# A selective scan with its partitions ordered state by state instead of channel by channel

## The chip, the cores and the metric

The kernel runs on one core of a Trainium2 chip, in float32 throughout. The metric is the device time of one execution in microseconds; less is better. A core has five engines with instruction streams of their own: PE multiplies matrices, ACT applies functions and copies, DVE and POOL work elementwise, SP issues DMAs here. They wait for each other through semaphores. Sixteen DMA engines move data between the on-chip memory (128 partitions) and DRAM.

## What is computed

Two layers on an input of [2, 256, 256, 128]: an attention over the first image axis, then a state space layer, each on a group-normalised input and added to its input. The change touches the second one alone. Cut to what matters (C = 128 channels, DI = 256 inner channels, 16 states, L = 65,536 positions per image):

```python
xi, z = split(gn(x) @ in_proj_w.T)                  # 256 channels each
xi = silu(depthwise_conv3x3(xi) + conv_b)           # xs, [B, 256, L]
dts, Bs, Cs = split(x_proj_w @ xs)                  # 8, 16 and 16 rows
delta = softplus(dt_w @ dts + dt_b)                 # [B, 256, L]
A = -exp(A_logs)                                    # [256, 16]
for t in range(L):                                  # per channel d and state n
    h[d, n] = exp(delta[d, t] * A[d, n]) * h[d, n] + delta[d, t] * xs[d, t] * Bs[n, t]
    y[d, t] = sum over n of h[d, n] * Cs[n, t]
y = y + Ds * xs
out = x + (layernorm(y) * ln_g + ln_b) * silu(z) @ out_proj_w.T
```

## The kernel before

**Stages.** After set-up and statistics comes attention; its result `x1` goes to DRAM. The scan stage then works through 128 steps (`steps`), 64 for each of two images; a step is R = 4 image rows, T = 1,024 positions.

**The partitions of a scan.** A step has 256 channels x 16 states = 4,096 recurrences of T positions, and one scan instruction runs 128 of them, one per partition. So a step has NU = 32 units: a unit takes CQ = 32 channels (one of four quarters `q` of one of two halves `h`) and SR = 4 states (one of four groups `m`). In the kernel before partition p holds channel p // 4 and state p % 4. Two units with neighbouring quarters form a pair (`PAIRS`, line 655). A pair's place in that tuple gives its time: unit t begins at slot t, and a step has 32 slots.

**Spreading the operands.** What the scan needs per partition is fetched from DRAM copies with repetition. `spread` (line 1154) fetches 32 channel rows of `delta_d` or `du_d` and repeats each for 4 states; `repeat` (line 1149) fetches 4 state rows of `bc_d` (B or C) and repeats them for 32 channels. Each such fetch fills a [128, 1024] tile. Per step there are 8 fetches of delta (`fetch_delta`, five buffers), 8 of du (`fetch_du`, two per tile, two buffers), 5 of B, 5 of C (`fetch_b`, `fetch_c`, two buffers each) and one of the fourth group of C (`fetch_cx`). All DMAs are issued by SP.

**The work of a unit.** `decay` (1229): ACT forms exp(delta x A), with A as a per-partition scale `a_neg`, in a PSUM tile `da`. `drive` (1241): POOL multiplies du and B for a pair at once. `scan` (1269): DVE runs the recurrence, with the end of the last step as its start. `remember` (1277): ACT keeps the last column. The product with C is made by DVE for single units (`product`, 1286) or by POOL for the eight pairs in `POOLED` (`products`, 1294). `add_up` (1316): PE sums over the 4 states with a 128 x 32 selection matrix `sel`, into 32 rows of `y`.

**The turned state group.** For the fourth group (`TURNED`) the drive is made another way, to spare POOL. `turn_du` (960) transposes du so that positions lie on partitions; `turn_du_out` (969) copies it into `zt`; `drives` (974) writes three copies of it scaled with B of one state each, the fourth being scaled through C. `turn_in` (1257) transposes 128 columns of `zt` back into `da`. `zt` is laid out as

```python
v["zt"] = s6.tile([P, T // P, DI, SR], F32, name="zt")
nc.scalar.copy(v["zt"][:, 2 * i : 2 * i + 2, :, SR - 1], o["ut", i])
```

so a copy of one state (256 elements, lines 976 to 981) reads and writes every fourth element, 16 bytes apart.

**Projecting ahead and finishing.** `project` (769) prepares a step up to 52 slots early: load four rows, `turn` and `normalise` them to channels on partitions (`xn`), `inner` and `conv`, `gate`, `silu`, `states`, `size`, `softplus`, `times`; it stores sz, xs, delta, du and B/C rows to DRAM. `begin` (793) keeps two rows of the step before or, on an image's first step, clears the row above the image, loads its first row into a tile `ob` and turns it; after the image's last row it clears a row. `finish_row` (1024) takes one of four rows of the step before through layer norm, gating, output projection and the store.

**The order.** Nothing is reordered by a scheduler in this stage: every piece has times in the table `TIMES` (line 661), in slots relative to the step's first unit, `at` (747) adds 32 slots per step, and all pieces are issued in the order of these times (lines 1385 to 1387). So each engine's stream, SP's too, is the order of the table.

**Set-up that depends on the partition order.** `sel` (152) sums the identity's columns in groups of 4. `same` (172), which has 1 where p % 32 = c, serves the convolution's weights. `A_logs` goes through a DRAM tile `alog_d` (190) in 32 small DMAs, to be read back with (channel, state) as partition.

Of the kernel before, what the change touches and what calls it, by code (L numbers as in the profile page):

```python
# [9 lines left out]
F32 = mybir.dt.float32  # L10
AF = mybir.ActivationFunctionType
ALU = mybir.AluOpType
AX = mybir.AxisListType
# [3 lines left out]
P = 128  # L17
# [5 lines left out]
def attn_then_ssm_kernel(  # L23
# [26 lines left out]
    nc = tc.nc  # L50
    B, H, W, C = x.shape
# [54 lines left out]
    first = ExitStack()  # L106
# [3 lines left out]
    for k in range(2):  # L110
# [40 lines left out]
    a_neg = const.tile([P, NCG, NSG], F32, name="a_neg")  # L151
    sel = const.tile([P, CQ], F32, name="sel")
    nc.vector.tensor_reduce(
        sel, ident.rearrange("p (c r) -> p c r", r=SR), AX.X, ALU.add
    )

    RB = TB // W
# [1 line left out]
    with tc.tile_pool(name="prep", bufs=1) as prep, tc.tile_pool(  # L159
# [7 lines left out]
        for r in range(RB):  # L167
            for dy in range(3):
                nc.sync.dma_start(
                    out=cw[(r + dy) * CQ : (r + dy + 1) * CQ, :, r, :], in_=taps[:, :, dy, :]  # L170
                )
        same = prep.tile([P, CQ], F32, name="same")
        nc.vector.tensor_reduce(
            same, ident.rearrange("p (r c) -> p c r", c=CQ), AX.X, ALU.add
        )
        nc.vector.tensor_tensor(
            w_cv.rearrange("p g r d c -> p (g r d) c"),
            same.unsqueeze(1).to_broadcast([P, NCG * RB * 3, CQ]),
            cw.rearrange("p g r d -> p (g r d)").unsqueeze(2).to_broadcast([P, NCG * RB * 3, CQ]),
            ALU.mult,  # L180
        )
# [5 lines left out]
        nc.sync.dma_start(out=xpw[32:64, :], in_=x_proj_w[0, DR : DR + 2 * NS, :])  # L187
        dtw = prep.tile([P, NH, DR], F32, name="dtw")
        nc.sync.dma_start(out=dtw, in_=dt_w[0].rearrange("(h p) r -> p h r", p=P))
        alog_d = dram.tile([CQ, SR, NCG, NSG], F32, name="alog_d")  # L190
        for g in range(NCG):
            for m in range(NSG):
                nc.sync.dma_start(
                    out=alog_d[:, :, g, m],
                    in_=A_logs[g * CQ : (g + 1) * CQ, m * SR : (m + 1) * SR],
                )
        alog = prep.tile([P, NCG, NSG], F32, name="alog")
        nc.sync.dma_start(out=alog, in_=alog_d.rearrange("c r g m -> (c r) g m"))
        a_pos = prep.tile([P, NCG, NSG], F32, name="a_pos")
        nc.scalar.activation(a_pos, alog, AF.Exp)  # L200
        nc.vector.tensor_scalar(a_neg, a_pos, -1.0, None, ALU.mult)
# [116 lines left out]
    with ExitStack() as actx:  # L318
# [268 lines left out]
        with tc.manual_schedule(engines=engines):  # L587
# [71 lines left out]
    POOLED = (2, 4, 10, 12, 18, 20, 26, 30)  # L659
    SUMS = ((0, 2), (4, 6), (8, 10), (12, 14), (16, 18), (20, 22), (24, 26), (28, 30))  # L660
    TIMES = {
        "add_up": (6.724, 10.523, 15.234, 17.357, 23.577, 27.066, 31.528, 34.187,),
        "begin": (-46.647,),
        "conv": (-37.319, -33.26, -30.256, -23.187,),
        "conv_out": (-37.203, -32.298, -29.079, -22.531,),
        "decay": (
            -0.457, -0.009, 1.46, 2.524, 2.97, 3.951, 4.748, 6.603, 7.256, 7.99, 7.7, 8.96, 9.084,
            7.786, 12.346, 13.841, 15.488, 16.811, 17.403, 14.296, 19.264, 20.338, 21.36, 21.952,
            23.923, 24.277, 25.955, 26.637, 26.688, 28.054, 29.215, 30.729,
        ),  # L670
        "drive": (
            -2.478, -0.654, 1.762, 3.81, 6.989, 11.716, 14.121, 17.755, 19.949, 23.283, 25.806,
            26.998,
        ),
        "drives": (
            -8.898, -8.755, 2.16, 8.854, -5.671, -4.828, -5.842, -1.931, -5.258, 3.165, -5.885,
            6.474, 2.13, 5.925, -3.57, 1.156,
        ),
        "fetch_b": (-4.274, -3.132, 4.233, 5.726, 22.495,),
        "fetch_c": (-2.23, 2.972, 5.721, 10.592, 28.034,),  # L680
        "fetch_cx": (-6.513,),
        "fetch_delta": (-9.068, -2.243, 0.347, -2.618, 11.064, 13.651, 5.759, 10.856,),
        "fetch_du": (-5.916, -3.021, 10.561, 13.429,),
        "gate": (-33.667, -30.07, -30.491, -26.072,),
        "gate_out": (-33.279, -28.439, -30.401, -25.691,),
        "inner": (-40.499, -39.775, -36.487, -34.84, -31.681, -31.179, -27.674, -24.89,),
        "inner_out": (-39.934, -39.214, -35.665, -34.411, -31.186, -30.784, -27.39, -23.412,),
        "load": (-52.341,),
        "normalise": (-43.293, -42.071,),
        "product": (  # L690
            0.814, 1.744, 6.726, 7.428, 8.79, 9.803, 15.226, 15.302, 17.41, 17.593, 23.225,
            23.505, 24.863, 25.246, 28.32, 29.93,
        ),
        "products": (5.397, 7.89, 14.546, 17.263, 21.546, 22.117, 27.902, 34.092,),
        "remember": (
            1.264, 2.345, 3.214, 6.053, 6.484, 7.988, 9.009, 9.1, 11.486, 14.169, 14.492, 15.761,
            17.254, 17.474, 20.057, 21.886, 23.549, 23.215, 25.088, 26.351, 27.149, 29.047,
            30.658, 32.752,
        ),
        "row_back": (41.992, 49.875, 57.857, 65.191,),  # L700
        "row_fetch": (43.062, 45.977, 52.544, 63.797,),
        "row_gated": (44.51, 49.95, 58.115, 65.232,),
        "row_leave": (45.329, 51.392, 61.182, 70.675,),
        "row_mix": (44.946, 51.011, 60.158, 69.774,),
        "row_norm": (41.251, 49.16, 55.004, 63.737,),
        "row_scales": (41.007, 47.422, 54.441, 63.428,),
        "row_stats": (39.857, 46.949, 53.374, 62.217,),
        "row_turn": (39.103, 45.623, 53.215, 61.229,),
        "silu": (-20.93,),
        "size": (-17.158, -16.246, -14.523, -14.865,),  # L710
        "size_out": (-16.533, -15.379, -13.973, -14.754,),
        "softplus": (-12.917,),
        "start_up": (-5.227, 19.105,),
        "start_up_y": (6.598, 23.449,),
        "states": (-20.725, -18.696,),
        "states_out": (-19.252, -17.616,),
        "times": (-11.031,),
        "turn": (-44.119, -42.473,),
        "turn_b": (-13.925,),
        "turn_b_out": (-12.571,),  # L720
        "turn_du": (-9.691, -6.021, -7.213, -4.676,),
        "turn_du_out": (-9.002, -5.843, -7.087, -4.562,),
        "turn_in": (9.374, 10.415, 10.881, 11.321, 17.974, 18.627, 19.701, 20.235,),
        "y_out": (20.647, 36.827,),
    }
    IN_F = {"gate": (0, 1, 0, 0), "turn_du": (2, 2, 2, 3)}
    s1 = ctx.enter_context(tc.tile_pool(name="s1", bufs=1))
# [41 lines left out]
    def project(k):  # L769
# [23 lines left out]
        def begin():  # L793
            if s == 0:
                if k > 0:
                    nc.gpsimd.memset(xn[:, 0, :], 0.0)
                first = s1.tile([P, WT, C], F32, name="ob")
                nc.sync.dma_start(
                    out=first, in_=x1[b][0].rearrange("(t p) c -> p t c", p=P)
                )  # L800
                o["first"] = first.unsqueeze(1)
                turn("first", 0, 1)
                normalise(1, 1)
            else:
                nc.scalar.copy(xn[:, 0:2, :], xn[:, R : R + 2, :])
            if n < R:
                nc.gpsimd.memset(xn[:, 2 + n, :], 0.0)

        def turn(src, r, m):
            t_ps = o["t"] = bank([P, RB, W], "t_ps")  # L810
            for i in range(m):
                for t in range(WT):
                    nc.tensor.transpose(
                        t_ps[:, i, t * P : (t + 1) * P], o[src][:, r + i, t, :], ident
                    )

        def normalise(to, m):
            nc.scalar.activation(
                xn[:, to : to + m, :],
                o["t"][:, 0:m, :],  # L820
                AF.Identity,
                bias=sh,
                scale=rs,
            )

        def inner(h, i, j, f=0):

# [140 lines left out]

        def turn_du_out(i):
            if i == 0:  # L970
                v["zt"] = s6.tile([P, T // P, DI, SR], F32, name="zt")
            nc.scalar.copy(v["zt"][:, 2 * i : 2 * i + 2, :, SR - 1], o["ut", i])  # L972

        def drives(j, n, m):
            for r in range(n, m):
                nc.scalar.activation(  # L976
                    v["zt"][:, j, :, r],
                    v["zt"][:, j, :, SR - 1],
                    AF.Copy,
                    scale=v["bt"][:, j, r : r + 1],  # L980
                )
# [167 lines left out]
    def repeat(k, name, row, m, pool):  # L1149
        tl = repeats[name, k, m] = pool.tile([P, T], F32, name=name[:3].rstrip("'"))  # L1150
        a = row + m * SR
        nc.sync.dma_start(out=tl, in_=given[k]["bc"][a : a + SR, :].partition_broadcast(CQ))

    def spread(k, name, tl, h, q):
        nc.sync.dma_start(
            out=tl,
            in_=given[k][name][h, q * CQ : (q + 1) * CQ, :]
            .unsqueeze(1)
            .to_broadcast([CQ, SR, T]),
        )  # L1160

    def fetch_b(k, m, again):
# [94 lines left out]
    def turn_in(t):  # L1257

        k, h, m, q = unit(t)
        da = units[t]["da"] = ps_d.tile([P, T], F32, name=f"da{t % 2}")  # L1260
        a = h * P + q * CQ
        for j in range(T // P):
            nc.tensor.transpose(  # L1263
                da[:, j * P : (j + 1) * P],
                given[k]["zt"][:, j, a : a + CQ, :].rearrange("p c r -> p (c r)"),
                ident,
            )

# [156 lines left out]
```

## Time and profile before

| | |
|---|---|
| time, median of 3 runs | 16,293.8 us (16,292.24 to 16,300.75) |
| the profiled execution's own time | 16,262.75 us |
| its span, first to last instruction | 16,261.0 us |
| mean granted TensorE clock | 0.926 |
| instructions | 265,160 |
| HBM read, written | 2,416.88 MB, 687.88 MB |
| DMA packets | 1,336,402, 3,122.11 MB |
| POOL's drives (L1244), 1,536 | 4,679 ns each |
| DVE's scans (L1275), 4,096 in three groups | 2,333 to 2,344 ns each |
| DVE's products (L1292), 2,048 | 1,219 ns each |

The prediction adds up busy times of one profiled execution and therefore starts from its time, which lies 0.19% under the median of the runs. "Busy" leaves out register, semaphore and DMA-issuing instructions. In lines with an arrow the written tile stands before it and the read ones behind it; "L976" is line 976 of the kernel before. The DMA share is the mean busy share of the core's 16 DMA engines.

### The profile page before, as it was taken

What the parts mean: (1) busy time and instruction counts of PE and PEld (TensorE: products, weight loads), DVE (VectorE), ACT (ScalarE), POOL (GpSimd) and SP (SyncE); (2) the same over time, 40 slices, a digit from 0 to 9 for tenths busy, and PEclk for the clock granted to TensorE, in tenths of its full rate; (3) what the DMA queues carried; (4) which work ended last, traced back from release to release, by engine and by line L of the source; (5) the groups of instructions that cost most, each with busy time, mean ns of one, the idle gap of its engine ahead of it and who ended that gap; (6) DMA issues with size and microseconds to landing.
All of it is one profiled execution on the core that took longest, in us unless ns stands there. A gap on an engine that the chain in (4) does not pass through costs nothing.

```text
span 16261.0 us, 265160 instructions
## 1 busy us (share of the span) xinstructions
PE 13681.8 (84%) x102443; PEld 8025.9 (49%) x102443; DVE 13663.5 (84%) x11479; ACT 13899.9 (85%) x24467; POOL 12670.3 (78%) x2960
## 2 busy tenths in 40 slices
PE   6999997888888888888888888888888888888887
PEld 5877884444444444444444444444444444444444
DVE  6665556888888888888888888888888888888888
ACT  3555557999999999999999999999999999999997
POOL 1111115999999999989899999999999989999988
PEclk9999998999999999999999999999999999999998
DMA  4322224565655666555666556665556566566664
GB/s 189 135 84 88 84 83 153 209 213 206 212 209 207 212 213 208 208 206 209 211 208 211 209 205 213 213 209 207 207 208 216 202 209 209 208 212 208 212 209 168
DMA packets 1336402, 3122.11 MB, mean 192 GB/s; under 512 B 108856, under 2 KB 700256, under 8 KB 1314656
## 3 DMA queue, kind: packets, MB, share of 16 engines
q1 hardware_dynamic: 1335136, 3105.15, 54.5%
q8 instruction: 804, 13.17, 0.3%
q14 instruction: 462, 3.78, 0.1%
HBM read 2416.88 MB, written 687.88 MB: 191 GB/s over the span
## 4 chain that ended last, share of the span: by engine, by line
ACT 44%; PE 24%; DVE 8%; issue 5%; DMA 1%; POOL 1%; SPq 0%; POOLq 0%; DVEq 0%; ACTq 0%
ACT zt L976 14%; ACT da L1237 10%; DVE work L1275 7%; PE y L1325 5%; PE u_ps L851 4%; PE dt_ps L916 4%; ACT work L1237 3%; ACT raw L844 3%; ACT zt L972 3%; PE o_ps L1104 2%; PE da L1263 2%; PE xi_ps L835 2%; ACT sz L891 2%; PE yt L1053 2%; PE xd_ps L898 1%
## 5 line engine op out<-in xcount | busy, mean ns | idle before, releaser
L1244 POOL TENSOR_TENSOR work<-du_r,bb 128x2048 f32<-128x2048 f32 x1536 | 7163.3, 4679 | 793.6 <-DVE da L1275 409.9
L1275 DVE TENSOR_TENSOR_SCAN da<-da,state,work 128x1024 f32<-128x1024 f32 x2048 | 4776.2, 2344 | 256.2 <-ACT da L1237 216.9
L1237 ACT ACTIVATE da<-delta_r,a_neg 128x1024 f32<-128x1024 f32 x3072 | 3430.6, 1119 | 82.0 <-DVE work L1275 47.4
L976 ACT ACTIVATE zt<-zt,bt 128x256 f32<-128x256 f32 x4096 | 3073.1, 787 | 37.6
L1292 DVE TENSOR_TENSOR work<-da,cc 128x1024 f32<-128x1024 f32 x2048 | 2465.1, 1219 | 495.7 <-ACT state L1282 261.4
L1275 DVE TENSOR_TENSOR_SCAN work<-da,state,work 128x1024 f32<-128x1024 f32 x1024 | 2388.8, 2343 | 478.8 <-ACT da L1237 469.7
L1297 POOL TENSOR_TENSOR work<-work,cc 128x2048 f32<-128x2048 f32 x512 | 2350.9, 4592 | 419.0 <-ACT state L1284 415.0
L851 PE MATMUL u_ps<-raw,w_cv 128*32 128x255 f32 (+1 forms) x24576 | 1819.8, 456 | 896.3 <-ACT raw L844 337.4
L1275 DVE TENSOR_TENSOR_SCAN work<-work,state,da 128x1024 f32<-128x1024 f32 x1024 | 2346.4, 2333 | 158.0 <-PE da L1263 132.6
L1297 POOL TENSOR_TENSOR work<-work,ccx 128x2048 f32<-128x2048 f32 x512 | 2318.3, 4552 | 19.1 <-ACT state L1284 17.8
L1325 PE MATMUL y<-work,sel 128*32 128x512 f32 x16384 | 2204.0, 641 | 15.0 <-POOL work L1297 15.0
L851 PEld LDWEIGHTS u_ps<-raw,w_cv 128*32 128x32 f32 x24576 | 864.8, 128 | 1867.3 <-ACT sz L891 434.9
L475 POOL TENSOR_TENSOR x1g<-xc,bo_all 128x512 f32<-128x512 f32 x256 | 316.2, 1276 | 1843.9 <-DVE stats L530 1835.8
L835 PE MATMUL xi_ps<-xn,w_in 128*32 128x256 f32 x16384 | 1164.9, 392 | 342.9 <-ACT raw L844 325.9
L425 ACT ACTIVATE e<-s_ps,nmx 128x256 f32<-128x256 f32 x1024 | 477.2, 476 | 970.1 <-DVE nmx L416 877.0
L1263 PE MATMUL da<-ident,zt 128*128 128x128 f32 x8192 | 1179.0, 291 | 25.5 <-ACT state L1282 22.0
L1237 ACT ACTIVATE work<-delta_r,a_neg 128x1024 f32<-128x1024 f32 x1024 | 1163.4, 1148 | 2.0 <-PE y L1325 0.3
L1325 PEld LDWEIGHTS y<-work,sel 128*32 128x32 f32 x16384 | 561.7, 115 | 1208.4 <-issue 1059.0
L1263 PEld LDWEIGHTS da<-ident,zt 128*128 128x128 f32 x8192 | 975.9, 149 | 326.1 <-DVE work L1275 107.5
L1053 PE MATMUL yt<-centre,ys 128*128 128x256 f32 x4096 | 1010.5, 390 | 127.3 <-ACT ob L1121 127.2
L835 PEld LDWEIGHTS xi_ps<-xn,w_in 128*32 128x32 f32 x16384 | 500.3, 111 | 1025.2 <-ACT raw L844 504.1
L1053 PEld LDWEIGHTS yt<-centre,ys 128*128 128x128 f32 x4096 | 738.2, 190 | 477.8 <-ACT ob L1121 285.8
(175 smaller groups left out, 22878.7 us busy)
## 6 DMA issues: line engine op xcount, KB each, us to landing
delta_r<-delta_d SPq DMA_DIRECT2D x1024, 512.0 KB, 6.2
du_r<-du_d SPq DMA_DIRECT2D x1024, 512.0 KB, 6.3
bb<-bc_d SPq DMA_DIRECT2D x640, 512.0 KB, 6.8
cc<-bc_d SPq DMA_DIRECT2D x640, 512.0 KB, 4.7
sz_d<-sz SPq DMA_DIRECT2D x128, 1024.0 KB, 4.1
xs_d<-xs SPq DMA_DIRECT2D x128, 1024.0 KB, 7.5
delta_d<-sz SPq DMA_DIRECT2D x128, 1024.0 KB, 5.0
du_d<-xs SPq DMA_DIRECT2D x128, 1024.0 KB, 6.2
```

Source lines behind the costliest of these rows:

```text
L835: nc.tensor.matmul(o["xi", j][r * CQ : (r + 1) * CQ, q, :], w_in[:, h, c : c + CQ], xn[:, i * RB + r, :], start=True, stop=True,)
L851: nc.tensor.matmul(o["u"][q * CQ : (q + 1) * CQ, r, a:z], w_cv[:, h * NQ + q, r, dx, :], o["xin"][:, q, a + dx - 1 : z + dx - 1], start=(i ...
L916: nc.tensor.matmul(o["dt"], w_dt[:, h, :], o["xd"][0:DR, i * TB : (i + 1) * TB], start=True, stop=True,)
L976: nc.scalar.activation(v["zt"][:, j, :, r], v["zt"][:, j, :, SR - 1], AF.Copy, scale=v["bt"][:, j, r : r + 1],)
L1053: nc.tensor.matmul(o["yt"][:, j, :], ys[k, h][:, t0 + j * P : t0 + (j + 1) * P], centre[:, (1 - h) * P : (1 - h) * P + DI], start=(h == 0) ...
L1237: nc.scalar.activation(da, spreads["delta", k, h, q], AF.Exp, scale=a_neg[:, g, m : m + 1])
L1244: nc.gpsimd.tensor_tensor(open_pair(t, time_of(k, "drive", DRIVEN.index(t % NU))), spreads["du", k, h, q], repeat_of("bb", t).unsqueeze(1) ...
L1263: nc.tensor.transpose(da[:, j * P : (j + 1) * P], given[k]["zt"][:, j, a : a + CQ, :].rearrange("p c r -> p (c r)"), ident,)
L1275: nc.vector.tensor_tensor_scan(u["h"], u[ins[0]], u[ins[1]], st, ALU.mult, ALU.add)
L1292: nc.vector.tensor_tensor(u["yc"], u["h"], repeat_of("cc", t), ALU.mult)
L1297: nc.gpsimd.tensor_tensor(hb, hb, repeat_of("cc", t).unsqueeze(1).to_broadcast([P, 2, T]), ALU.mult)
L1325: nc.tensor.matmul(y[q * CQ : (q + 1) * CQ, cols], sel, units[u]["yc"][:, cols], start=False, stop=last,)
```

## The change

Partition p of a scan now holds state p // 32 and channel p % 32. What follows from it: `sel` becomes the matrix that was `same`, which goes; `alog_d`, `repeat` and `spread` have the state outermost; `zt` has runs of 32 channels per state, and the unit's 128 columns lie in the new order; the transposes read 128 neighbouring columns as before. Besides, `begin` gives its first-row load and its clearing of the row after the image to `normalise`, behind the activations of the loaded rows, and all times in `TIMES` are new. The parts of the diff:

```diff
-        sel, ident.rearrange("p (c r) -> p c r", r=SR), AX.X, ALU.add
+        sel, ident.rearrange("p (r c) -> p c r", c=CQ), AX.X, ALU.add
...
-        alog_d = dram.tile([CQ, SR, NCG, NSG], F32, name="alog_d")
+        alog_d = dram.tile([SR, CQ, NCG, NSG], F32, name="alog_d")
...
-                    in_=A_logs[g * CQ : (g + 1) * CQ, m * SR : (m + 1) * SR],
+                    in_=A_logs[g * CQ : (g + 1) * CQ, m * SR : (m + 1) * SR].rearrange("c r -> r c"),
...
-            -2.478, -0.654, 1.762, 3.81, 6.989, 11.716, 14.121, 17.755, 19.949, 23.283, 25.806,
-            26.998,
+            -0.699, 1.903, -0.246, 5.26, 7.3, 9.679, 10.621, 16.712, 16.704, 16.586, 24.816,
+            25.892,
...
-        "fetch_du": (-5.916, -3.021, 10.561, 13.429,),
+        "fetch_du": (-5.779, -0.439, 9.381, 12.598,),
...
         def begin():
             if s == 0:
                 if k > 0:
                     nc.gpsimd.memset(xn[:, 0, :], 0.0)
-                first = s1.tile([P, WT, C], F32, name="ob")
...
-                turn("first", 0, 1)
-                normalise(1, 1)
             else:
                 nc.scalar.copy(xn[:, 0:2, :], xn[:, R : R + 2, :])
-            if n < R:
-                nc.gpsimd.memset(xn[:, 2 + n, :], 0.0)
...
+            if s == 0 and to == 2:
+                first = s1.tile([P, WT, C], F32, name="ob")
...
+                turn("first", 0, 1)
+                normalise(1, 1)
+            if n < R and to == 2 + RB:
+                nc.gpsimd.memset(xn[:, 2 + n, :], 0.0)
...
-                v["zt"] = s6.tile([P, T // P, DI, SR], F32, name="zt")
-            nc.scalar.copy(v["zt"][:, 2 * i : 2 * i + 2, :, SR - 1], o["ut", i])
+                v["zt"] = s6.tile([P, T // P, NCG, SR, CQ], F32, name="zt")
+            nc.scalar.copy(
+                v["zt"][:, 2 * i : 2 * i + 2, :, SR - 1, :],
+                o["ut", i].rearrange("p j (g c) -> p j g c", c=CQ),
+            )
...
                 nc.scalar.activation(
-                    v["zt"][:, j, :, r],
-                    v["zt"][:, j, :, SR - 1],
+                    v["zt"][:, j, :, r, :],
+                    v["zt"][:, j, :, SR - 1, :],
                     AF.Copy,
                     scale=v["bt"][:, j, r : r + 1],
                 )
...
-        nc.sync.dma_start(out=tl, in_=given[k]["bc"][a : a + SR, :].partition_broadcast(CQ))
+        nc.sync.dma_start(out=tl, in_=given[k]["bc"][a : a + SR, :].unsqueeze(1).to_broadcast([SR, CQ, T]))
...
             in_=given[k][name][h, q * CQ : (q + 1) * CQ, :]
-            .unsqueeze(1)
-            .to_broadcast([CQ, SR, T]),
+            .unsqueeze(0)
+            .to_broadcast([SR, CQ, T]),
...
-                given[k]["zt"][:, j, a : a + CQ, :].rearrange("p c r -> p (c r)"),
+                given[k]["zt"][:, j, g, :, :].rearrange("p r c -> p (r c)"),
```

## The prediction

> **What bounds the kernel now.** I read the page first (busy shares, the 40 slices), then the busy time by stretch, then the chain of waits for one step, then the groups by cost, and last the DMA issues with the DMA rate in short windows, because the change rewrites DMA source patterns as well as copies.
>
> ```profile
> PE 13681.8 (84%) x102443; PEld 8025.9 (49%) x102443; DVE 13663.5 (84%) x11479; ACT 13899.9 (85%) x24467; POOL 12670.3 (78%) x2960
> ...
> DMA  4322224565655666555666556665556566566664
> ```
>
> The slices show two stages: six slices of attention, then the scan, flat to the end. The busy time by stretch (length, then PE, PE load, DVE, ACT, POOL busy, TensorE clock, DMA share, GB/s) gives the scan alone:
>
> ```profile
> 6000.00:9000.00 3000.00, 2496.15 (x19653) 1352.87 (x19646) 2662.90 (x1467) 2754.05 (x4593) 2719.70 (x593) 0.92 0.60 209
> ```
>
> The chain of waits repeats itself with one scan step; the squares of one row's statistics start at (start us, us, what):
>
> ```profile
> 8024.58 0.81 ACT yn L1065 x4
> ...
> 8130.49 0.81 ACT yn L1065 x4
> ...
> 8236.53 0.81 ACT yn L1065 x4
> ```
>
> Two periods are 211.95 us, so a step takes 106.0 us; 128 steps are 13,565 us, and the rest of the 16,261.0 us span, 2,696 us, is attention, filling and draining. Of each 106.0 us, ACT is busy 97.3 (2754.05/3000 x 106), POOL 96.1, DVE 94.1, PE 88.2, the DMA engines 63.6 (0.60). Four engines lie within 10% of each other; the chain over the whole span gives ACT the most (44%), and its largest line is the scaled copy:
>
> ```profile
> ACT 44%; PE 24%; DVE 8%; issue 5%; DMA 1%; POOL 1%; SPq 0%; POOLq 0%; DVEq 0%; ACTq 0%
> ACT zt L976 14%; ACT da L1237 10%; DVE work L1275 7%; PE y L1325 5%; PE u_ps L851 4%; PE dt_ps L916 4%; ACT work L1237 3%; ACT raw L844 3%; ACT zt L972 3%; PE o_ps L1104 2%; PE da L1263 2%; PE xi_ps L835 2%; ACT sz L891 2%; PE yt L1053 2%; PE xd_ps L898 1%
> ```
>
> DMA is 1% of the chain: now it is cover, with 42 us to spare per step. The reader should see that this holds only while all 16 engines share the load. The issues (count, KB each, us to landing):
>
> ```profile
> delta_r<-delta_d SPq DMA_DIRECT2D x1024, 512.0 KB, 6.2
> du_r<-du_d SPq DMA_DIRECT2D x1024, 512.0 KB, 6.3
> bb<-bc_d SPq DMA_DIRECT2D x640, 512.0 KB, 6.8
> cc<-bc_d SPq DMA_DIRECT2D x640, 512.0 KB, 4.7
> ...
> ccx<-bc_d SPq DMA_DIRECT2D x128, 512.0 KB, 3.8
> ```
>
> These are 3,456 fetches, 27 per step: 27 x 524,288 B = 14.16 MB of the 22.2 MB (209 GB/s x 106.0 us) that a step moves. And the rate when nearly all engines are busy, a stretch with a cc and a bb fetch in flight, one later in the step, and one of attention's loads:
>
> ```profile
> 8042.00:8044.00 2.00, 1.26 (x14) 0.65 (x7) 2.00 (x2) 1.97 (x5) 2.00 (x1) 1.00 0.98 389
> 8078.00:8080.00 2.00, 2.00 (x18) 0.48 (x10) 1.75 (x3) 1.60 (x3) 1.64 (x1) 1.00 1.03 418
> 60.00:100.00 40.00, 0.00 (x0) 0.00 (x0) 34.42 (x106) 0.00 (x0) 0.00 (x0) 1.00 1.01 430
> ```
>
> Per engine: 389/(0.98 x 16) = 24.8, 25.4 and 26.6 GB/s.
>
> **What the Trainium skill says.** (1) "DMA: Bandwidth & Descriptors", section "Why a DMA increments its semaphore by 16 and not by 1": the hardware generator looks at the slowest dimension (size above 1) of each side's pattern and uses the largest number of engines, at most 16, that divides both; it takes the lowest-numbered ones. (2) The same page, "Rules for kernel authors": "an outermost dim of size c < 16 — e.g. a leading zero-stride broadcast of c copies — confines the whole DMA to at most c engines". The kernel before has 32 outermost in these five fetches (128 on the tile's side), so 16 engines; that agrees with the 0.98 above, but no trace here shows a large DMA with a small outer dimension. (3) "ScalarE: Activation LUTs", section "What ACT_TABLE_LOAD costs", prices an ACTIVATE at 186 ns + 0.833 ns per element, 93 ns more per pointer operand: 492 ns for 256 elements with a pointer scale. L1077, that shape with contiguous operands, takes 473 ns; L976 takes 787. (4) "SBUF — State Buffer", section "Specifications (TRN2)": 16-byte lines, at least two hits on one needed for full rate. L976 steps 16 bytes between elements, one hit per line, which fits the 295 ns above the price.
>
> **The change part by part.** The groups by cost, over the 5,000 us from 5,000 us on (count, busy us, mean ns of one, idle before it):
>
> ```profile
> L976 ACT ACTIVATE zt<-zt,bt 128x256 f32<-128x256 f32 x1504 | 1127.6, 787 | 13.8
> ...
> L844 ACT COPY raw<-xi_ps 128x512 f32<-128x512 f32 x376 | 219.1, 583 | 17.2 <-PE xi_ps L835 15.2
> ...
> L972 ACT COPY zt<-ut_ps 128x512 f32<-128x512 f32 x188 | 201.9, 1074 | 40.2 <-PE ut_ps L965 40.2
> ...
> L1077 ACT ACTIVATE yn<-yt,rstd 128x256 f32<-128x256 f32 x376 | 156.7, 473 | 0.0
> ```
>
> *Copies in runs of 32.* Bounds for L976: 473 (L1077) to 787 (nothing gained). I take 490, the skill's price; a loss is excluded, since it does the same elements with fewer line changes. 32 per step x 0.297 = 9.5 us. L972 writes the same stride; its contiguous twin L844 takes 583, so 4 x 0.49 = 2.0 us. ACT goes from 97.3 to 85.8 us per step. By itself this makes POOL (96.1) and DVE (94.1) late next: at most 10 us can be won.
>
> *The fetches.* `repeat` now reads [4 rows, 32 copies, T], `spread` [4 copies, 32 rows, T]. Same count, bytes, tiles, issuing queue; but the outermost dimension is 4, so by (1) each runs on 4 engines, always the lowest four. Bounds: nothing (16 engines kept) to all 27 confined. I take all: both patterns have 4 first. Then each of those four moves 14.16/4 = 3.54 MB per step, at 25 GB/s 141.6 us, against 14.16/16/25 = 35.4 us now. The other DMAs stay spread: 63.6 - 35.4 = 28.2 us on every engine. The four lowest are busy 141.6 + 28.2 = 169.8 us per step, above any compute engine. DMA sets the pace, ACT's 11.5 us fall into idle time, and the timetable can't hide it: it changes order, not bytes.
>
> *Gaps in the four engines.* SP issues in order and waits for buffers and for stores to DRAM to land before their copies are fetched. Compute has 96 us of work in 170, so buffers come free early; some landings will leave the four queues empty. None: 0. All four stores that a fetch depends on (bc_d 6.3, delta_d 5.0, xs_d 7.5, du_d 6.2 by the DMA issues): 25 us. I take 8. Step: 178 us. At 26.6 GB/s without gaps it is 133.0 + 26.5 = 160; with all gaps 195.
>
> *The timetable.* SP, POOL, ACT, DVE and PE all follow the new times. POOL issues the same 21 operations per step and SP the same DMAs. One place looks tight: the third du fetch stands at 9.381, its first drive at 10.621, 1.24 slots of 3.31 us = 4.1 us, where two du loads land 6.3 us after issue (before: 10.561 and 14.121, 11.8 us). Behind that drive POOL's later products wait, and for those the add-ups. Bounds on 16 engines: from 5 us won (ACT's room used) to 3.4 us lost (6.3 + 1.2 issue - 4.1). Under DMA's pace: 0.
>
> *Edits with one answer.* The selection matrix, A's layout, the transposes at L1263 and the add-ups keep shape and count: 0. The dropped reduction and the 32 small A loads are in set-up, long before the first decay: under 10 us even if exposed. Moving the first row's load and the clearing behind the normalisation of the loaded rows concerns the first and last step of an image: that load lands after 4.8 us, so PE, with the next step's projections queued behind, may wait 2 x 5 = 10 us; the clearing stays on POOL (0.3 us).
>
> **The sum.** 2,696 + 128 x 178 = 25,480 us of span, with the 1.75 us around it (16,262.75 the profiled execution). The median of the runs shown, 16,293.8, is 0.19% above; I say 25,500.
>
> **Rivals.**
> - *Four engines, DMA bound* (forecast): for it the pattern's order and the skill's sentence; against it that no trace here shows the rule. Chance 0.83, 23,200 to 27,700 by the bounds above.
> - *Only `spread` confined* (its leading dimension is the zero-stride one; `repeat` leads with real rows). 16 fetches on four: 83.9 us, 11 on sixteen: 14.4, others 28.2: 126.5, with 5% of gaps 133: 2,696 + 128 x 133 = 19,720. Chance 0.05.
> - *The fetches keep 16 engines* (the other side): the place is the source pattern; if the generator splits by the tile's 128 partitions alone, L976's saving decides. POOL's 96.1 at today's ratio of the busiest engine (97.3/106.0 = 0.918) gives 104.7, at 0.95 101.2; I take 103: 15,880, faster. It decides once a fetch spreads over about 8 engines or more: 8 engines give 70.8 + 28.2 = 99 us. Chance 0.09.
> - *Sixteen engines and a timetable that gives it back*: POOL's wait above, 109.4 us per step: 16,700. Chance 0.02; within 0.2% (about what a measurement of this kernel can tell from no change) 0.01.
>
> **Numbers.** Faster 0.09, same 0.01, slower 0.90. The range must leave out no more than 2 in 10: the likeliest case widened beyond its bounds for gaps larger than I priced (215 us per step is 30,200, taken as rare), 22,700 to 29,300.
>
> **What would show it.** Right: DMA share in the scan near (4 x 0.95 + 12 x 0.16)/16 = 0.36 and 125 GB/s where 0.60 and 209 stand; fetches landing far later than 6 us; DVE, ACT and POOL waiting on delta_r, du_r, bb and cc; every compute engine near half busy; HBM bytes unchanged; L976 near 490 ns. Wrong: landings of 4 to 7 us and a DMA share of 0.6 would show 16 engines; L976 still at 787 would show that the stride was not its price, and would not change the time.

## The result, and the profile after

The changed kernel takes 25,125.7 us (median of 4 runs, 25,117.0 to 25,133.1) against 16,293.0 us beside it: 1.542 times as long (95% interval 1.540 to 1.545). Its profiled span is 25,115.3 us. The page of the changed kernel: busy time by engine, then the DMA engines' busy share in the 40 slices (in tenths).

```profile
PE 14872.8 (59%) x102443; PEld 8334.0 (33%) x102443; DVE 13714.0 (55%) x11478; ACT 12752.1 (51%) x24467; POOL 12545.1 (50%) x2960
...
DMA  4222333333333333333333333333333333333333
```

Attention fills the first four slices and is as before; all slices of the scan show the same low share. No compute engine carries the time: in the busy time by stretch (columns as before the change) all four are about half busy.

```profile
6000.00:9000.00 3000.00, 1666.06 (x11889) 858.98 (x11887) 1625.84 (x893) 1516.94 (x2786) 1623.92 (x357) 0.74 0.36 127
```

The DMA engines are not busy on average either: 0.36 where there was 0.60. That average is the trap of this case. With the 2,696 us outside the steps taken over, a step takes (25,115.3 - 2,696)/128 = 175.1 us, and for most of it a window of the trace looks like these three, from one stretch of 64 us:

```profile
12064.00:12068.00 4.00, 4.00 (x36) 1.27 (x28) 3.03 (x3) 2.22 (x6) 3.62 (x2) 0.75 0.26 104
12100.00:12104.00 4.00, 0.00 (x0) 0.00 (x0) 0.00 (x0) 0.00 (x0) 0.00 (x0) 0.93 0.26 103
12124.00:12128.00 4.00, 0.00 (x0) 0.00 (x0) 0.15 (x1) 1.30 (x2) 4.00 (x2) 0.50 0.25 102
```

A share of 0.25 to 0.26 at 102 to 104 GB/s is four engines of sixteen, busy throughout at 25.75 GB/s each; in the middle line no compute engine does anything. Over six steps read in windows of 1 us, the share lies between 0.18 and 0.32 in 70% of them, and under 0.05 in 4.5%; before, these were 2% and 29%. Counted packet by packet, exactly four DMA packets are in flight for 64% of the time from 9,000 to 12,000 us, and for 0.6% of it before.

The chain of waits has turned from ACT to DMA, and partly to SP's instruction stream (SPq):

```profile
DMA 47%; ACT 13%; PE 12%; SPq 12%; DVE 3%; issue 2%; POOL 1%; ACTq 0%; DVEq 0%; POOLq 0%
```

In time, single fetches stand on it for over 20 us, where a fetch landed some 6 us after its issue before (start, us, what):

```profile
9015.51 20.65 DMA delta_r<-delta_d
9113.34 23.59 DMA delta_r<-delta_d
...
9193.56 20.15 DMA delta_r<-delta_d
```

One fetch alone, 0.52 MB at 103 GB/s, would take 5.1 us; 20 us fit several in flight that share the same four engines. Which four they are, the trace doesn't say. SP is held too: in six steps its issuing instructions take 2.4 us each on average, 115 us of a step, where they took 0.6 us each and 28 us of a step before.

Who waited for whom, 9,000 to 12,000 us (us in total, times, longest): POOL waits for du, ACT for delta, DVE for ACT and for C.

```profile
POOL work L1244 <- DMA du_r<-du_d: 1083.6, 68, 23.4
ACT da L1237 <- DMA delta_r<-delta_d: 608.8, 68, 15.9
DVE da L1275 <- ACT da L1237: 446.2, 65, 19.3
DVE work L1292 <- DMA cc<-bc_d: 344.1, 30, 19.8
```

The copies did get short. The groups by cost, 10,000 to 15,000 us, with the columns used before; L969 is what was L972:

```profile
L976 ACT ACTIVATE zt<-zt,bt 128x256 f32<-128x256 f32 x910 | 425.6, 502 | 7.4
...
L1077 ACT ACTIVATE yn<-yt,rstd 128x256 f32<-128x256 f32 x226 | 93.7, 467 | 0.9
...
L969 ACT COPY zt<-ut_ps 128x512 f32<-128x512 f32 x112 | 65.8, 587 | 71.3 <-PE ut_ps L962 71.3
```

787 ns have become 502, and 1,074 have become 587. ACT works 88.5 us per step instead of 97.3 (1516.94/3000 x 175.1); while DMA sets the pace, that hardly shows in the time.

### The profile page after: what moved, and what is told of

Its sections match the earlier page's. It is cut to its first block, busy times and chain, and to the rows that moved or that the text cites. A ratio compares the mean times of both kernels' runs of the same rounds, so it can differ in the third digit from the quotient of the medians.

```text
span 25115.3 us, 265032 instructions
## 1 busy us (share of the span) xinstructions
PE 14872.8 (59%) x102443; PEld 8334.0 (33%) x102443; DVE 13714.0 (55%) x11478; ACT 12752.1 (51%) x24467; POOL 12545.1 (50%) x2960
## 4 chain that ended last, share of the span: by engine, by line
DMA 47%; ACT 13%; PE 12%; SPq 12%; DVE 3%; issue 2%; POOL 1%; ACTq 0%; DVEq 0%; POOLq 0%
DMA delta_r<-delta_d 22%; DMA sz_d<-sz 10%; DMA xr<-xs_d 7%; DMA cc<-bc_d 6%; PE u_ps L848 5%; SPq L1155 5%; ACT da L1237 3%; ACT work L1237 2%; SPq L1122 2%; PE y L1314 2%; PE y L1325 2%; ACT zt L976 2%; SPq L909 2%; SPq L1152 1%; PE xi_ps L832 1%
## 5 line engine op out<-in xcount | busy, mean ns | idle before, releaser
L1244 POOL TENSOR_TENSOR work<-du_r,bb 128x2048 f32<-128x2048 f32 x1536 | 7048.8, 4602 | 9562.0 <-DMA du_r<-du_d 7893.7
L848 PE MATMUL u_ps<-raw,w_cv 128*32 128x255 f32 (+1 forms) x24576 | 1691.3, 431 | 1999.3 <-ACT sz L888 1873.8
L1325 PE MATMUL y<-work,sel 128*32 128x512 f32 x16384 | 2641.8, 712 | 302.1 <-POOL work L1297 301.2
L1297 POOL TENSOR_TENSOR work<-work,cc 128x2048 f32<-128x2048 f32 x512 | 2329.8, 4550 | 561.1 <-ACT state L1284 561.1
L1297 POOL TENSOR_TENSOR work<-work,ccx 128x2048 f32<-128x2048 f32 x512 | 2308.2, 4520 | 133.1 <-ACT state L1284 131.5
L832 PE MATMUL xi_ps<-xn,w_in 128*32 128x256 f32 x16384 | 1293.5, 441 | 1281.6 <-ACT raw L841 785.4
L976 ACT ACTIVATE zt<-zt,bt 128x256 f32<-128x256 f32 x4096 | 1914.4, 502 | 33.3
L877 PE MATMUL z_ps<-xn,w_z 128*128 128x512 f32 x1024 | 783.5, 858 | 1581.0 <-DVE yn L1096 1560.6
L913 PE MATMUL dt_ps<-xr,w_dt 8*128 8x512 f32 x1024 | 751.7, 821 | 1605.3 <-ACT sz L924 1602.3
L1282 ACT COPY state<-da 128x1 f32<-128x1 f32 x2048 | 317.2, 155 | 1782.4 <-DVE work L1292 1644.4
```

The source lines that it names most:

```text
L832: nc.tensor.matmul(o["xi", j][r * CQ : (r + 1) * CQ, q, :], w_in[:, h, c : c + CQ], xn[:, i * RB + r, :], start=True, stop=True,)
L848: nc.tensor.matmul(o["u"][q * CQ : (q + 1) * CQ, r, a:z], w_cv[:, h * NQ + q, r, dx, :], o["xin"][:, q, a + dx - 1 : z + dx - 1], start=(i ...
L877: nc.tensor.matmul(o["z", h, i], w_z[:, h, :], xn[:, 1 + i * RB : 1 + (i + 1) * RB, :], start=True, stop=True,)
L976: nc.scalar.activation(v["zt"][:, j, :, r, :], v["zt"][:, j, :, SR - 1, :], AF.Copy, scale=v["bt"][:, j, r : r + 1],)
L1244: nc.gpsimd.tensor_tensor(open_pair(t, time_of(k, "drive", DRIVEN.index(t % NU))), spreads["du", k, h, q], repeat_of("bb", t).unsqueeze(1) ...
L1297: nc.gpsimd.tensor_tensor(hb, hb, repeat_of("cc", t).unsqueeze(1).to_broadcast([P, 2, T]), ALU.mult)
```

## The experiments

Theory: the new source patterns, with 4 outermost, put each fetch on four engines. Its rivals: the new timetable costs the time; or the order does, in which DRAM rows are read (under `repeat` one row now 32 times in a row). Some kernels below compute other values, where their expectation says so; their work has the same shape. The ratio behind each time is to the kernel before, measured beside it, with its 95% interval.

**Both patterns alone, and both put back.** In the kernel before:

```diff
-        ... in_=given[k]["bc"][a : a + SR, :].partition_broadcast(CQ))
+        ... in_=given[k]["bc"][a : a + SR, :].unsqueeze(1).to_broadcast([SR, CQ, T]))
...
-            .unsqueeze(1)
-            .to_broadcast([CQ, SR, T]),
+            .unsqueeze(0)
+            .to_broadcast([SR, CQ, T]),
```

> The kernel before with only the two source patterns of repeat and spread changed (state outermost); copies, layout and timetable are the old ones, so the scan's operands no longer fit its A and selection matrix: the scan computes other values of the same shape. Four engines: 14.16 MB / 4 / 25.7 GB/s (the rate in the changed kernel's trace, 103 GB/s over four) = 137.7 us, others 28.4, gaps 9: 175 us per step, 25,100 us (24,600 to 25,800). If the new timetable costs the time: 16,290 to 17,000.

Measured: 25,363.3 us, 1.557 (1.555 to 1.559). The same lines in the other direction, in the changed kernel:

> The changed kernel with only these two source patterns put back (channels outermost), so the scan computes other values. Four engines: all 16 work again and the copies' saving shows, 15,900 us (15,700 to 16,200), the scaled copy still at 502 ns. If the timetable costs the time: above 20,000, as the changed kernel. If the timetable has no use for ACT's room: 16,260 or more.

Measured: 15,843.7 us, 0.972 (0.971 to 0.974). The busy time by stretch of this kernel:

```profile
9000.00:12000.00 3000.00, 2505.11 (x20265) 1320.39 (x20266) 2753.89 (x1517) 2570.21 (x4754) 2809.03 (x615) 0.95 0.62 217
```

DMA share and rate are again those of sixteen engines, and POOL is busy 94% of the time. So the two patterns carry the whole loss; without them the rest of the change takes 2.8% off, in a kernel that computes other values. The timetable is not what costs the time.

**Each pattern alone**, in the kernel before:

> The kernel before with only spread's source changed (16 of the 27 fetches; the scan computes other values). Four engines: 8.39 MB / 4 / 25.7 = 81.6 us, the other 11 fetches 14.0, others 28.4: 124 busy, gaps 9: 133 us per step, 19,700 us (19,000 to 20,400). If reading one DRAM row many times in a row is what is slow, spread (which now passes over 32 different rows) costs nothing: 16,300.

> The kernel before with only repeat's source changed (11 of the 27 fetches, each row now read 32 times in a row; the scan computes other values). Four engines: 5.77 MB / 4 / 25.7 = 56.1 us, the other 16 fetches 20.4, others 28.4: 105 busy, about what the compute engines take (106): with gaps 114 us per step, 17,300 us (16,400 to 18,000). If repeated rows are what is slow: all of the loss is here, 25,000.

Measured: 22,795.2 us, 1.399 (1.397 to 1.402), and 19,200.4 us, 1.179 (1.177 to 1.181). Both patterns lose, in the order that their bytes on four engines give, so reading one row many times isn't the cause: `spread` passes over 32 rows and costs more. But both sizes were missed. A step takes 157.0 and 128.9 us; the busy time worked out for the four engines is 124 and 105, so 33 and 24 us are left over, where all 27 fetches on four leave 9. The stretches of the two, `spread` first:

```profile
6000.00:9000.00 3000.00, 1844.56 (x13256) 1014.25 (x13255) 1805.16 (x992) 1867.84 (x3103) 1830.22 (x402) 0.79 0.45 141
```

```profile
6000.00:9000.00 3000.00, 2168.04 (x16123) 1174.55 (x16125) 2200.71 (x1208) 2268.99 (x3781) 2236.72 (x488) 0.85 0.53 173
```

About half of what is left over is idle time: all DMA engines rest (share under 0.05 in windows of 1 us) for 12% and 10% of the time, some 19 and 13 us of a step. What makes these gaps is not shown. SP's longest wait, for POOL's products (L1297) to free a buffer, is 35 us per step with `spread` alone (670.9 us in 19 steps), but it is 31 in the kernel before too; SP's issuing instructions take 79 us of a step with `spread` alone and 28 before. The other half fits slower transfers: the share of `spread` alone is 0.45 x 16 x 157.0 = 1,130 us of engine time per step, summed over the engines, where the terms of the expectation give 1,005 (4 x 81.6 and 16 x 42.4), and a packet of 4 KB takes 204 ns on average, against 174 in the changed kernel and 183 before. Why it takes longer stays open.

**The same order on 16 and on 2 engines.** In the changed kernel, each fetch as DMAs of one state (shown), or of two:

```diff
-        nc.sync.dma_start(out=tl, in_=...["bc"][a : a + SR, :].unsqueeze(1).to_broadcast([SR, CQ, T]))
+        for r in range(SR):
+            nc.sync.dma_start(
+                out=tl[r * CQ : (r + 1) * CQ, :],
+                in_=given[k]["bc"][a + r : a + r + 1, :].to_broadcast([CQ, T]),
+            )
...
+        for r in range(SR):
+            nc.sync.dma_start(
+                out=tl[r * CQ : (r + 1) * CQ, :],
+                in_=given[k][name][h, q * CQ : (q + 1) * CQ, :],
+            )
```

> The changed kernel, computing the same, with every fetch as four DMAs of one state (32 partitions each, 32 rows or 32 copies outermost). Bytes, rows and partitions are those of the changed kernel; only the outermost count goes from 4 to 32. Four engines: all 16 work, and the time falls to that of the patterns put back plus what 81 more issues per step cost SP (108 x 0.55 = 59 us of a step of 103, still under it): 15,950 us (15,800 to 16,300). If the order of rows and partitions is what is slow: 25,000 or more.

> The changed kernel, computing the same, with every fetch as two DMAs of two states (2 outermost, 64 partitions). Four engines, taken to two: 14.16 MB / 2 / 25.7 GB/s = 275.4 us on each of the two lowest, others 28.4, gaps 9: 313 us per step, 42,750 us (41,500 to 44,000). If it is the order of rows, or too few DMAs in flight: 25,100 or less.

Measured: 16,633.5 us, 1.022 (1.020 to 1.023), and 41,772.8 us, 2.565 (2.561 to 2.570). Which row goes to which partition is the same in both and in the changed kernel. The count outermost differs, and with it the number of DMAs and the partitions of each; since two DMAs per fetch lose and four win, it is not their number that costs. With 2 outermost, windows of the trace show the next step down:

```profile
15096.00:15104.00 8.00, 8.00 (x68) 3.93 (x61) 4.86 (x3) 6.15 (x13) 5.61 (x2) 0.75 0.14 53
15120.00:15128.00 8.00, 3.43 (x34) 0.97 (x33) 4.66 (x3) 2.63 (x4) 0.00 (x0) 0.93 0.13 52
```

0.13 to 0.14 is two engines of sixteen (2/16 = 0.125), at 26 to 26.5 GB/s each; exactly two packets are in flight for 81% of the time from 9,000 to 12,000 us. So 2, 4 and 16 engines give 41,773, 25,126 and 15,844 us (the last with the patterns put back), and the changed order itself gives 16,633 when no fetch has fewer than 32 outermost: this settles the number of engines as the cause, and the order of rows falls.

The kernel with one-state fetches is free of the four engines but misses its expectation by 680 us. Its stretch:

```profile
9000.00:12000.00 3000.00, 2414.55 (x19050) 1261.86 (x19047) 2587.50 (x1425) 2421.74 (x4455) 2633.91 (x580) 0.91 0.77 203
```

Share 0.77 at 203 GB/s is 16.5 GB/s per busy engine, where the kernel before has 21.8 (209/0.60/16). With four DMAs of 32 partitions per fetch the engines are busy longer for the same bytes. SP's issuing takes 74 us of a step of 108.8, under the step as expected. How the 680 us divide between the two is not shown.

**What the 2.8% are made of.** In the kernel before, the runs alone (the layout of `zt` and its readers), and the timetable alone:

```diff
-                v["zt"] = s6.tile([P, T // P, DI, SR], F32, name="zt")
+                v["zt"] = s6.tile([P, T // P, NCG, SR, CQ], F32, name="zt")
...
-                    v["zt"][:, j, :, r],
-                    v["zt"][:, j, :, SR - 1],
+                    v["zt"][:, j, :, r, :],
+                    v["zt"][:, j, :, SR - 1, :],
```

> The kernel before with only the turned state group's copies in runs of 32, with their transposes; fetches, A and selection matrix keep the old order, so the turned units compute other values. Timetable as before. The copies take 11 us of ACT per step less. If ACT's queue carries the time: 16,000 us (15,850 to 16,150). If POOL and DVE take over at once, or the gain needs the new timetable: 16,284 within 0.3%.

> The kernel before with only the new timetable (with the moved first-row load and clearing), computing the same. If the timetable alone won what the patterns put back showed: 15,900. If it was made for short copies and ACT still has its 97 us per step: 16,300 to 16,600; I expect 16,400.

Measured: 15,948.3 us, 0.980 (0.979 to 0.982), and 16,330.6 us, 1.003 (1.002 to 1.004). The runs carry the gain; the timetable (with the moved first-row load and clearing) costs 0.3% with long copies and gives a further 0.7% with short ones (15,948 to 15,844). In the stretch of the timetable alone ACT is still the busiest engine (2733.66 of 3000):

```profile
9000.00:12000.00 3000.00, 2431.41 (x19516) 1285.72 (x19512) 2658.79 (x1459) 2733.66 (x4570) 2702.18 (x593) 0.93 0.60 208
```

**A version that keeps part of the gain.** A pattern with 16 outermost and still some run: partition p holds channel 2 x (p // 8) + p % 2 and state (p // 2) % 4. Copies write runs of two; a fetch is two DMAs of every second partition.

```diff
+                v["zt"] = s6.tile([P, T // P, DI // 2, SR, 2], F32, name="zt")
...
+        for l in range(2):
+            nc.sync.dma_start(
+                out=tl[l : P : 2, :],
+                in_=given[k]["bc"][a : a + SR, :].partition_broadcast(CQ // 2),
+            )
...
+        for l in range(2):
+            nc.sync.dma_start(
+                out=tl[l : P : 2, :],
+                in_=given[k][name][h, q * CQ : (q + 1) * CQ, :]
+                .rearrange("(x l) t -> l x t", l=2)[l]
+                .unsqueeze(1)
+                .to_broadcast([CQ // 2, SR, T]),
+            )
```

> The changed kernel, computing the same, with another partition order: 16 groups of (4 states x 2 channels), so that the turned group's copies write runs of two elements, and every fetch is two DMAs of 64 partitions with 16 outermost. Four engines: all 16 work (DMA share 0.6 to 0.75 in the scan), no wait for fetches worth naming; if two hits on a line are enough, the scaled copy takes 502 ns and the time is between the patterns put back (15,844) and the kernel with one-state fetches (16,633), which lost to small DMAs: 16,000 us (15,850 to 16,250). If a run of two is still slow, the copy stays near 787 ns and the time is 16,350 to 16,600.

Measured: 16,192.7 us, 0.995 (0.994 to 0.996): within what I had expected, at its slow end. The copies in the groups by cost (9,000 to 12,000 us; L986 and L979 are the scaled and the plain copy here):

```profile
L986 ACT ACTIVATE zt<-zt,bt 128x256 f32<-128x256 f32 x896 | 443.3, 531 | 7.3
...
L979 ACT COPY zt<-ut_ps 128x512 f32<-128x512 f32 x112 | 71.2, 635 | 65.1 <-PE ut_ps L972 65.0
```

A run of two gets most of the way: 531 ns against 502 in runs of 32. My "no wait for fetches worth naming" was wrong, as POOL's largest wait shows (L1260 is its drive here):

```profile
POOL work L1260 <- DMA du_r<-du_d: 235.6, 64, 8.6
```

Over 28.4 steps of 105.5 us that is 8 us per step. Two remedies for it, the old timetable, and two entries of the new one changed:

```diff
-        "fetch_du": (-5.779, -0.439, 9.381, 12.598,),
+        "fetch_du": (-5.779, -2.2, 8.35, 12.598,),
```

> The kernel with runs of two and two DMAs per fetch, with the timetable of the kernel before. In the new timetable POOL waits 8 us per step for the late du fetches; the old one has 11.8 us between the third du fetch and its drive: if that wait is what holds the kernel with runs of two, 16,050 us (15,950 to 16,150). If the new timetable is the better one here too, as it is with one DMA per fetch (15,844 against 15,948 with the old one): 16,300.

> The kernel with runs of two and the new timetable, with two entries changed: the second du fetch at -2.2 instead of -0.439, the third at 8.35 instead of 9.381. If their lateness makes POOL's wait: 16,050 us (15,950 to 16,130). If the buffer, free only after the drive at 7.3, or the busy queues set it: 16,190 within 0.3%.

Measured: 16,619.1 us, 1.020 (1.018 to 1.022), and 16,123.2 us, 0.990 (0.988 to 0.991). Neither brought what the wait had promised. With the entries moved POOL's wait halves, but DVE's wait for C grows from 33.2 us to 152.1 (L1308 is its product):

```profile
DVE work L1308 <- DMA cc<-bc_d: 152.1, 29, 7.0
POOL work L1260 <- DMA du_r<-du_d: 117.0, 51, 4.4
```

POOL waits 4 us less per step, and the time falls by 0.55% by the two ratios, some 0.6 us per step: inside the expected range, near its slow end. The old timetable was a miss. It halves POOL's wait as well (118.5 us), yet DVE waits longer still for C (L1307 is its product):

```profile
DVE work L1307 <- DMA cc<-bc_d: 228.9, 28, 11.0
```

The kernel with runs of two and the two entries computes the same as the kernels before and after, and takes 1.0% less than the one before.

## Why the prediction was right

- *What bounds.* "DMA sets the pace, ACT's 11.5 us fall into idle time": shown by the two patterns alone (1.557) and put back (0.972), and by the step from 16 to 4 to 2 engines.
- *The sum, term by term.* Step: 178 predicted, 175.1 measured. Fetches on four engines: 141.6 at 25 GB/s; the three windows above have 25.75, which makes 137.4. Other DMAs: 28.2; from the share, 0.36 x 16 x 175.1 = 1,009 engine-us, less 4 x 137.4, over 16 is 28.7. Gaps: 8; what is left is 9.0. The rate of an engine, put 3% too low by these windows, makes the forecast 4.2 us per step too long; the other two terms take 1.5 us of that back. So the 1.5% between forecast and result owes a little to errors that cancel. DMA share and rate in the scan were forecast as 0.36 and 125 GB/s; they are 0.36 and 127.
- *The copies.* 490 ns predicted, 502 measured; 583 and 587. The skill's price (page "ScalarE: Activation LUTs", section "What ACT_TABLE_LOAD costs"), 492 ns, was within 2%, and its rule of two hits on a line (page "SBUF — State Buffer", section "Specifications (TRN2)") nearly holds here: 787 ns with one hit, 531 with two, 502 with all four.
- *The timetable, "under DMA's pace: 0".* Nearly: with the old copies and times the two patterns give 25,363, 0.9% more than the changed kernel, 2 us per step. The rest of the change is worth that much even under the four engines.
- *The rival on the other side*, 16 engines with a step of 103 and 15,880 us, was right as arithmetic: with the patterns put back the step is 102.4 and the time 15,844. Its condition failed.
- *The tight du fetch.* Seen at the right place: with the patterns put back POOL waits 154.0 us for du in 29.3 steps, 5.3 per step. Before, it was 31.7 us in 28.3 steps, 1.1 per step. But the rival that made a loss of it (109.4 us per step) was wrong: with that wait in it the step is 102.4, shorter than the 106.0 before.
- *The rival with `spread` alone* was mis-sized: 19,720 predicted, 22,795 measured. The term that failed is "with 5% of gaps" over a busy time of 126.5: 33 us lie above the busy time of 124 worked out from the measured rate, some 19 of them idle, the others fitting slower packets. Where all 27 fetches are on four engines, 9 us are left over. Why a mixture leaves more is not shown.

## What to carry to other kernels

A DMA's bytes, count and tile say nothing of how many engines carry it: look at the outermost count of its source pattern, the side that was varied here, above all when a repetition moves to the front. A low mean DMA share is no proof that DMA is idle: read it in windows of a few microseconds beside its rate, for a plateau at 4/16 or 2/16. And a layout chosen for one engine's access pattern has to be priced on every transfer that fills it; here runs of two, with 16 still outermost, shortened the copies nearly as much as runs of 32 (531 ns against 502), but the split fetches left 1.0% of the time to win, where 2.8% stood with the fetches untouched.

## What the runs showed that I had not expected

- Fetches split into DMAs of fewer partitions cost engine time: 21.8 GB/s per busy engine with 128 partitions per DMA (before), 18.2 with two DMAs of every second partition (210 GB/s at 0.72), 16.5 with four of 32. These are means over all DMAs of a step, not of the fetches alone.
- In the windows shown, one DMA engine moves 26 to 26.5 GB/s where two work, 25.5 to 26 where four do, and 24.8 to 26.6 where nearly all sixteen do (the prediction's three windows): no order by their number shows.
- TensorE's mean granted clock was low where the time was long: 0.66 at 41,773 us, 0.76 at 25,126, 0.926 before, 0.95 with the patterns put back. Near the time of before the two don't go together (0.94 at 16,619 us, 0.92 at 16,633). PE was busy 97 us of a step in the changed kernel where it was busy 88 before (1666.06/3000 x 175.1); its part of the chain fell from 24% to 12%.
